# Two graph layers on one core: another order of head sums, V products, key dots and the load of x on VectorE

## The chip, the cores and the metric

The kernel runs on one core of one Trainium2 chip. The metric is device microseconds of one execution. All arithmetic is float32. The engines are called as the profile calls them: PE is TensorE (PEld its weight loads), DVE VectorE, ACT ScalarE, POOL GpSimd, SP SyncE, which here only issues DMAs. Each engine works through its own instructions strictly in the order in which they are written; between engines, semaphores make an instruction wait for what it needs.

## What is computed

64 graphs of 256 nodes with 512 features go through two layers:

```python
# layer 0: one head
feat = einsum('bnh,oh->bno', x, fc_w) + fc_b
q, k = feat . q_w + q_b, feat . k_w + k_b
masked = leaky_relu(q + k^T + (1 - adj) * -1e9, 0.01)
x1 = einsum('bnm,bmh->bnh', softmax(masked), feat) + x
# layer 1: eight heads of 64
Q, K, V = x1 @ W_q + b_q, x1 @ W_k + b_k, x1 @ W_v + b_v
scores = Q K^T / 8 + a[i] + c[j] + b_g + log(adj + 1e-9)     # a, c: x1 . w_g
out = softmax(scores) V + x1
```

## The kernel before

Two graphs (512 tokens) make a group; there are 32 groups. The loop at the end (from line 1155) takes one `step` a group, and each step works on three to four groups at once: `f`, whose features of layer 1 are computed now; `a`, the group before it, which is in its attention (scores, softmax, weighted sum); `d`, the one before that, whose last outputs leave; and `n`, the next, whose x and adj are loaded and whose layer-0 weights are prepared. The order of everything is written out by hand: a step is a list of strings such as `A("both:0 parts:0")`, where the letter names the group and each word a method with its arguments. The order of the words is the order on every engine that a method uses.

What matters for the change:

- **Block products.** The 512x512 products with the weights (Q, K, V as `pq`, `pk`, `pv`, and `pf` in layer 0) are each made of seven products of half blocks instead of eight (class `Product`, lines 383 to 468). `p1` opens an accumulator in PSUM; ACT copies it out (`keep_1`). `p6` and `p5` add to it, and each time ACT copies it out again (`s2`, `s4`); `p3` adds to it once more and ACT reads the block of the result. `p2` opens one of its own, and `p7` a third. DVE makes the other three blocks of the result: `sum_00` from p2 and the first copy, `sum_11` from p7 and `s4`, `sum_10` from the third after `p4` has added to it, and `s2`. So `p4` may only add when `sum_11` has read the third accumulator, and `p3` only when ACT has copied `s4`. All matmuls of these products have line 404, the sums line 432, the copies 418 and 421.
- **Tokens' sums.** `xsum:0` to `xsum:3` (line 369, tile t1b) and in layer 0 `ysum:0` to `ysum:3` (line 344, tile tb) are the differences of blocks that products 5, 6, 7 and 4 take. `copy:n` are copies on ACT.
- **Head sums.** In attention each of the four units u (graph, half of the heads) has two tiles e of exponentials. `both:u` (line 875) adds them into one tile `es`, `parts:u` transposes it into `est` (line 904) and reduces it to partial row sums (line 905). `est` takes the buffer e0, which also holds the layer-0 weights of the next group in another part of the step. `totals`, `ratios` (line 926), `turn` (966), `divide` (986), `complete` (994) and `store` (1027) finish an output of one graph; `turn_residual` (832) transposes the residual into `xb`, which has two buffers, freed when the stores from it have landed.
- **x and adj.** x has one buffer. The four `keys` dots (line 508, jc) are the last readers of x of the group f; then `load_x` (line 200) fetches x of the group n, and its first readers are the four `dot_q` (jq). `spread` sends the results through DRAM and back to all partitions (qrow), for `weights:0` and `weights:1` (lines 593, 597, and the exponential on ACT, line 598), which make the layer-0 weights in e0. adj has one buffer, filled at the start of a step in four DMAs (line 195) and read by `adjt` (line 551) in its last third; ACT makes the mask from it (lines 559, 560).
- **x1 transposed.** As each quarter of x1 is done (line 490), `send` (lines 781, 785) transposes it in blocks and writes it to DRAM, and `fetch` (line 793) reads it back in four DMAs as x1T, which Q, K and V are made from.
- **PSUM.** There are eight banks; the scores (line 850) of a step use all eight twice, and each takes a bank that an earlier tile has left.

Of the kernel before, what the change touches and what calls it, by code (L numbers as in the profile page):

```python
# [10 lines left out]
F32 = mybir.dt.float32  # L11
# [6 lines left out]
P = 128  # L18
# [7 lines left out]
def kernel(  # L26
# [65 lines left out]
    NB, N, D = x.shape  # L92
# [4 lines left out]
    NC = D // P  # L97
# [15 lines left out]
    both = [i for i, a in enumerate(act_sets.SETS) if a.name == "natural_log_exp_and_others"]  # L113
    nc.scalar.add_instruction(
        mybir.InstLoadActFuncSet(
            name=nc.get_next_instruction_name(), act_func_set_id=both[0], ins=[], outs=[]
# [47 lines left out]
    def fast():  # L164
        main = ExitStack()
        with main:
            one = main.enter_context(tc.tile_pool(name="one", bufs=1))
# [350 lines left out]
            class Group:  # L518
# [378 lines left out]
                def parts(self, u):  # L897

                    g, (gr, hg), nb = self.g, divmod(u, 2), NC * N // B
                    if hg == 0:  # L900
                        self.part_all = two.tile([P, ALL], F32, tag="part", name=f"part_{g}_{gr}")
                        self.part = self.part_all[:, 0 : 2 * nb].rearrange("p (a m) -> p a m", a=2)
                    turned = one.tile([P, NC * N], F32, tag="e0", name=f"est_{g}_{u}")
                    nc.vector.transpose(turned, self.esum[u].rearrange("p a b i -> p (a b i)"))  # L904
                    nc.vector.tensor_reduce(  # L905
                        self.part[:, hg, :], turned.rearrange("p (m c) -> p m c", c=B),
                        AX.X, ALU.add,
                    )
# [137 lines left out]
            def attention_and_layer_0(D, A, F, X):  # L1046

                A("scores:0 scores:1 scores:2 scores:3")
                F("add_tiles parts_0")
                A("factor:0:0 factor:0:1 factor:1:0 factor:1:1")  # L1050
                A("factor:2:0 factor:2:1 factor:3:0 factor:3:1")
                F("mix:0 mix:1 recip mix:2 mix:3 ysum:0")
                D("ratios:1 divide:1")
                A("residual:1")
                F("ysum:1")
                D("complete:1 store:1")
                F("ysum:2 pf.p1 pf.keep_1 pf.p2 pf.p6 pf.sum_00 begin send:0:0 fetch:0:0 ysum:3")
                A("turn_residual:1 both:0 parts:0")
                F("pf.p7 pf.p5 pf.p3 pf.add_01 pf.sum_11 send:1:1")
                A("attend:0")  # L1060
                F("pf.sum_01 send:0:1 fetch:1:1 fetch:0:1")
                A("both:1 turn:0 attend:1 parts:1")
                F("copy:0 pf.p4 pf.sum_10 send:1:0 fetch:1:0")
                F("pq.p1 pq.keep_1 pk.p1")
                A("totals:0")
                F("pk.keep_1 pv.p1 pv.keep_1")

            def check_ranges():

                in_range(NG - NR // 2, NG, "last")  # L1070
                pk = bank("pok")
                nc.tensor.transpose(pk[0:1, 0:P], checked["all"], ident)

                def flag_ready():
                    oks = one.tile([1, 2], F32, tag="oks", name="oks")
                    nc.vector.tensor_reduce(oks[:, 0:1], pk[0:1, 0:P], AX.X, ALU.min)
                    nc.vector.tensor_copy(flag, oks[:, 0:1])

                return flag_ready
# [3 lines left out]
            def step(d, a, f, n, check):  # L1083


                def of(group):
                    def issue(pieces):
                        for piece in pieces.split():
                            name, *args = piece.split(":")
                            if group is None:  # L1090
                                continue
                            target = group
                            if "." in name:
                                part, name = name.split(".")
                                target = getattr(group, part)
                            getattr(target, name)(*map(int, args))
                    return issue

                D, A, F, X = of(d), of(a), of(f), of(n)
                f.older = d  # L1100
                X("load_adj")
                if a is not None:
                    attention_and_layer_0(D, A, F, X)
                else:
                    f.features_first()
                    F("pq.p1 pq.keep_1 copy:0 pk.p1 pk.keep_1 pv.p1 pv.keep_1")
                F("xsum:0 xsum:1 xsum:2 pq.p6")
                A("ratios:0 both:2 parts:2")
                F("keys:2 keys:3 keys:0 keys:1")
                X("load_x")  # L1110
                F("pq.p7 pq.p2 pq.sum_00 xsum:3")
                check()
                F("pq.p5 pk.p6 pq.sum_11 pq.p3")
                A("divide:0")
                X("dot_q:0 dot_q:1 dot_q:2 dot_q:3 spread")
                F("pq.p4 pq.sum_10 copy:1 copy:2")
                A("complete:0 store:0 turn:1 both:3 parts:3")
                F("pk.p7 pk.p5 pk.sum_11 residual:0")
                X("adjt")
                F("pk.p2 pk.sum_00")  # L1120
                X("dot_k:0 dot_k:1")
                F("pk.p3 pk.p4 pk.sum_10")
                X("dot_k:2 dot_k:3")
                F("turn_residual:0")
                if n is None:
                    A("totals:1 ratios:1 divide:1 complete:1 store:1")
                    F("residual:1 turn_residual:1")

                    F("pv.p2 pv.p6 pv.sum_00 scores:0 scores:1 scores:2 scores:3")
                    F("pv.p7 factor:0:0 factor:0:1 factor:1:0 factor:1:1 both:0 both:1")  # L1130
                    F("pv.p5 pv.sum_11 pv.p3 sums_1:0 pv.p4 pv.sum_10")
                    F("factor:2:0 factor:2:1 ratios_t:0 ratios_r:0 factor:3:0 factor:3:1")
                    F("attend:0 finish:0 sums_of_e:1 attend:1")
                    F("ratios_t:1 ratios_r:1 finish:1")
                    check_ranges()()
                    return
                X("mask add_eps")
                F("pv.p2 pv.p6")
                X("weights:0")
                F("pv.p7 pv.p5")  # L1140
                X("weights:1")
                F("pv.sum_00 pv.p3 pv.sum_11 pv.p4 pv.sum_10")

            with tc.manual_schedule(engines=ENGINES):
                f = Group(0)
                f.x, f.a = x_0, adj_0

                warm = bank("warm")
                for n in range(6):
                    nc.tensor.matmul(warm[:, 0:P], lhsT=ident, rhs=ident, start=True, stop=True)  # L1150
                columns(rows_0, cols_0, "cols_0")
                rows_qk = rows_of_x()
                k_constant = constant()
                d, a, a_w = None, None, {}
                for g in range(NG):
                    n = Group(g + 1) if g + 1 < NG else None

                    def check():

                        if d is not None and (d.g % NR == NR - 1 or d.g == NG - NR // 2 - 1):  # L1160
                            in_range(d.g // NR * NR, d.g + 1, f"{d.g}")

                    step(d, a, f, n, check)
                    d, a, f = a, f, n
# [215 lines left out]
```

## Time and profile before

| what | value |
|---|---|
| median of three runs | 2486.52 us |
| lowest, highest | 2484.86, 2499.46 us |
| profiled execution: device time | 2491.2 us |
| its span, first to last instruction | 2489.4 us |
| its granted TensorE clock, mean | 0.983 |
| DMA, mean over the span | 66 GB/s |

The costliest groups of the page, for the durations (line, engine, operation, result and operands, shapes, count; busy us, mean ns of one; idle time before them and what ended it):

```profile
L867 DVE TENSOR_TENSOR e<-e,am 128x1024 f32<-128x1024 f32 x256 | 293.4, 1218 | 0.0
L404 PE MATMUL pk<-t1b,wk 128*128 128x256 f32 x512 | 147.2, 438 | 92.7 <-DVE kT L432 92.7
L904 DVE STREAM_TRANSPOSE est<-es 128x1024 f32<-128x1024 f32 x124 | 153.1, 1235 | 3.2
L905 DVE TENSOR_REDUCE part<-est 128x32 f32<-128x1024 f32 x124 | 151.3, 1220 | 4.2
L875 DVE TENSOR_TENSOR es<-e,e 128x1024 f32<-128x1024 f32 x126 | 152.6, 1212 | 0.4
L508 DVE CUSTOM_DVE_ANT_0 jq<-x,wq_row 128x512 f32<-128x512 f32 x128 | 88.5, 692 | 51.1 <-DMA x<-in_x_dram 47.8
```

The granted clock is the share of its full speed that the TensorE was given. Ends of matmuls are modelled; their starts tell more. An idle time is put down to whatever came last.

### The profile page before, as it was taken

Reading aid. Unit: us, or ns where it says so; the run is one execution under the profiler, and the core shown is the slowest. Engines: PE = TensorE matmul, PEld = TensorE weight load, DVE = VectorE, ACT = ScalarE, POOL = GpSimd, SP = SyncE. Lnnn points to the kernel's source line nnn. Section 1 sums busy time; section 2 is a strip of 40 time slices with the busy share of each in tenths; the row PEclk is TensorE's granted clock in tenths of the full one; section 3 lists DMA queues with packets and bytes.
Section 4 is the critical chain, followed back from the end, with each engine's and each line's share of the span. In section 5 each row is a group of like instructions: output and inputs, shape, how many; then the busy total and the mean of one; then the engine's idle time right before and its main releaser. Section 6 shows DMA issues by size and latency. Waiting matters only on the chain.

```text
span 2489.4 us, 33742 instructions
## 1 busy us (share of the span) xinstructions
PE 2338.5 (94%) x12554; PEld 1924.0 (77%) x12554; DVE 2155.1 (87%) x3212; ACT 1086.1 (44%) x2121; POOL 130.4 (5%) x120
## 2 busy tenths in 40 slices
PE   9999999999999999999999999999999999999997
PEld 6877777777787777877777877778777787777875
DVE  6788888888888898888889888898988988889897
ACT  3444344443444443444434444344444344443443
POOL 0000000000000000000000000000000000000000
PEclk9999999999999999999999999999999999999999
DMA  4122322223322223222232222322222322223222
GB/s 123 47 56 64 81 67 57 56 64 81 75 66 56 60 68 81 67 58 56 64 81 68 55 61 58 81 74 67 60 60 64 81 63 61 55 64 81 66 50 36
DMA packets 517266, 163.85 MB, mean 66 GB/s; under 512 B 415188, under 2 KB 478696, under 8 KB 517096
## 3 DMA queue, kind: packets, MB, share of 16 engines
q1 hardware_dynamic: 514440, 160.32, 27.1%
q8 instruction: 101, 1.65, 0.3%
q10 hardware_dynamic: 2656, 1.31, 0.2%
q14 instruction: 69, 0.57, 0.1%
HBM read 95.43 MB, written 66.12 MB: 65 GB/s over the span
## 4 chain that ended last, share of the span: by engine, by line
PE 45%; DVE 34%; DMA 12%; issue 3%; SPq 3%; ACT 1%; DVEq 0%; POOL 0%; ACTq 0%; POOLq 0%
PE pv L404 11%; PE y L678 9%; PE sc L850 9%; PE pf L404 7%; DMA x<-in_x_dram 7%; DVE est L904 4%; DVE es L875 4%; DVE jq L508 3%; PE pk L404 3%; DVE part L905 3%; DVE x L490 2%; PE pq L404 2%; SPq L793 2%; DMA xd<-xt 2%; PE oT L888 2%
## 5 line engine op out<-in xcount | busy, mean ns | idle before, releaser
L859 ACT ACTIVATE e<-sc,c 128x512 f32<-128x512 f32 x512 | 299.3, 735 | 69.9 <-PE sc L850 69.9
L867 DVE TENSOR_TENSOR e<-e,am 128x1024 f32<-128x1024 f32 x256 | 293.4, 1218 | 0.0
L484 POOL TENSOR_TENSOR pf_s<-pf_s,x 128x512 f32<-128x512 f32 x93 | 126.9, 1364 | 2274.8 <-ACT pf_s L483 2217.5
L404 PE MATMUL pk<-t1b,wk 128*128 128x256 f32 x512 | 147.2, 438 | 92.7 <-DVE kT L432 92.7
L850 PE MATMUL sc<-qT,kT 64*128 64x256 f32 x2048 | 230.7, 380 | 0.0
L888 PE MATMUL oT<-e,v 128*64 128x256 f32 x2048 | 230.0, 383 | 0.0
L678 PE MATMUL y<-e,x 128*128 128x256 f32 x992 | 228.8, 384 | 0.0
L850 PEld LDWEIGHTS sc<-qT,kT 64*128 64x128 f32 x2048 | 196.1, 187 | 32.4 <-issue 10.6
L678 PEld LDWEIGHTS y<-e,x 128*128 128x128 f32 x992 | 183.6, 190 | 32.7 <-ACT e L859 10.3
L888 PEld LDWEIGHTS oT<-e,v 128*64 128x64 f32 x2048 | 144.9, 138 | 81.1 <-issue 12.5
L404 PEld LDWEIGHTS pk<-t1b,wk 128*128 128x128 f32 x512 | 108.7, 218 | 121.8 <-DVE kT L432 105.2
L895 ACT COPY oTs<-oT 128x512 f32<-128x512 f32 x128 | 71.9, 587 | 262.1 <-DVE osb L966 133.6
L421 ACT ACTIVATE pq_s<-pq,cols 128x256 f32<-128x256 f32 x192 | 80.5, 471 | 238.9 <-DVE qT L432 126.5
L904 DVE STREAM_TRANSPOSE est<-es 128x1024 f32<-128x1024 f32 x124 | 153.1, 1235 | 3.2
L905 DVE TENSOR_REDUCE part<-est 128x32 f32<-128x1024 f32 x124 | 151.3, 1220 | 4.2
L875 DVE TENSOR_TENSOR es<-e,e 128x1024 f32<-128x1024 f32 x126 | 152.6, 1212 | 0.4
L483 ACT ACTIVATE pf_s<-pf,recip 128x256 f32<-128x256 f32 x186 | 77.4, 467 | 153.3 <-PE pf L404 153.3
L432 DVE TENSOR_TENSOR v<-pv,pv_s 128x512 f32<-128x512 f32 x96 | 64.1, 687 | 89.7 <-PE pv L404 84.9
L508 DVE CUSTOM_DVE_ANT_0 jq<-x,wq_row 128x512 f32<-128x512 f32 x128 | 88.5, 692 | 51.1 <-DMA x<-in_x_dram 47.8
L404 PE MATMUL pv<-wv,t1b_c 128*128 128x256 f32 x512 | 131.8, 403 | 0.0
L818 ACT ACTIVATE xv<-x1T,cols 128x256 f32<-128x256 f32 x256 | 109.1, 498 | 50.1 <-DVE osb L966 46.2
L418 ACT COPY pk_s<-pk 128x512 f32<-128x512 f32 x96 | 56.3, 586 | 168.5 <-PE pk L404 95.3
(175 smaller groups left out, 4597.0 us busy)
## 6 DMA issues: line engine op xcount, KB each, us to landing
x<-in_x_dram SPq DMA_DIRECT2D x32, 1024.0 KB, 5.1
xd<-xt SPq DMA_DIRECT2D x124, 256.0 KB, 2.0
x1T<-xd SPq DMA_DIRECT2D x496, 64.0 KB, 2.0
out_dram<-xb SPq DMA_DIRECT2D x248, 128.0 KB, 3.1
adj<-in_adj_dram SPq DMA_DIRECT2D x128, 128.0 KB, 3.6
qrow<-q SPq DMA_DIRECT2D x31, 256.0 KB, 4.0
fc_nat<-in_L_gnn_fc_w_dram ACTq DMA_DIRECT2D x4, 256.0 KB, 4.4
wq<-in_L_gnn_W_q_dram SPq DMA_DIRECT2D x1, 1024.0 KB
```

The lines of the kernel that those rows point to most:

```text
L404: nc.tensor.matmul(o, lhsT=lk[:, ts(m, P)] if len(lk.shape) == 2 else lk[:, m], rhs=rk, start=(start and m == 0 and k == 0), stop=(m == 1 ...
L484: nc.gpsimd.tensor_tensor(s, s, self.out(o, k), ALU.add)
L508: nc.vector.tensor_tensor_reduce(out=junk, in0=src, in1=w_row, scale=1.0, scalar=init, op0=ALU.mult, op1=ALU.add, accum_out=dst,)
L678: nc.tensor.matmul(y[:, ts(gr, N)], lhsT=self.x[:, gr * TPG + j, ts(c, P)], rhs=self.e0[:, j, gr, :], start=(gr == 0 and j == 0), stop=(gr ...
L818: nc.scalar.activation(self.xv[:, c].rearrange("p (t a m) -> p t a m", t=TPG, m=B), self.x1T[:, c // 2, gr].rearrange("p (a t c m) -> p c ...
L850: nc.tensor.matmul(sc[par][:, pr, :], lhsT=self.kT[rows, 2 * hg + pr, ts(t, P)], rhs=self.qT[rows, 2 * hg + pr, ts(gr, N)], start=True, st ...
L859: nc.scalar.activation(e[:, par], sc[par], AF.Exp, bias=self.c[:, t : t + 1], scale=SCALE)
L867: nc.vector.tensor_tensor(ef, ef, self.am[:, jc, u // 2, :].unsqueeze(1).to_broadcast([P, 4, N]), ALU.mult,)
L875: nc.vector.tensor_tensor(self.esum[u], self.e[u, 0], self.e[u, 1], ALU.add)
L888: nc.tensor.matmul(oT[par * HD : (par + 1) * HD, pr, :], lhsT=self.v[:, gr * TPG + jc, ts(h, HD)], rhs=self.e[2 * gr + hg, jc][:, par, pr, :],
L904: nc.vector.transpose(turned, self.esum[u].rearrange("p a b i -> p (a b i)"))
L905: nc.vector.tensor_reduce(self.part[:, hg, :], turned.rearrange("p (m c) -> p m c", c=B), AX.X, ALU.add,)
```

## The change

Four things move in the step; no instruction is added or taken away. The sum of the last head unit, `both:3 parts:3`, goes from its place behind `turn:1` (ahead of pk.sum_11) to the end of the step, between pv.sum_00 and pv.sum_10; in the last step, which has no next group, it stays where it was. Since e0 holds the next group's layer-0 weights by then, its transposed tile takes the buffer of adj instead. The key dots and the load of x go ahead of `ratios:0 both:2 parts:2`. The V products run as 6 7 5 2 3 4 instead of 2 6 7 5 3 4, with their sums in the order 11, 00, 10. And `turn_residual:1` goes behind `both:0 parts:0`.

```diff
-                    turned = one.tile([P, NC * N], F32, tag="e0", name=f"est_{g}_{u}")
+                    tag = "adj" if u == 3 else "e0"
+                    turned = one.tile([P, NC * N], F32, tag=tag, name=f"est_{g}_{u}")
...
-                A("turn_residual:1 both:0 parts:0")
+                A("both:0 parts:0 turn_residual:1")
...
-                A("ratios:0 both:2 parts:2")
                 F("keys:2 keys:3 keys:0 keys:1")
                 X("load_x")
+                A("ratios:0 both:2 parts:2")
                 F("pq.p7 pq.p2 pq.sum_00 xsum:3")
...
-                A("complete:0 store:0 turn:1 both:3 parts:3")
+                A("complete:0 store:0 turn:1")
+                if n is None:
+                    A("both:3 parts:3")
                 F("pk.p7 pk.p5 pk.sum_11 residual:0")
...
                 X("mask add_eps")
-                F("pv.p2 pv.p6")
+                F("pv.p6 pv.p7")
                 X("weights:0")
-                F("pv.p7 pv.p5")
+                F("pv.p5 pv.p2")
                 X("weights:1")
-                F("pv.sum_00 pv.p3 pv.sum_11 pv.p4 pv.sum_10")
+                F("pv.sum_11 pv.p3 pv.p4 pv.sum_00")
+                A("both:3 parts:3")
+                F("pv.sum_10")
```

## The prediction

> **What bounds the kernel now.** The page's engine totals come first: PE is busy for 94% of the span, so most of the time is matmul and a change of order on VectorE can only win what PE spends waiting. So I read the waits of PE next, then the timelines at the longest one.
>
> ```profile
> PE 2338.5 (94%) x12554; PEld 1924.0 (77%) x12554; DVE 2155.1 (87%) x3212; ACT 1086.1 (44%) x2121; POOL 130.4 (5%) x120
> ```
>
> The waits of PE (total us, times, longest) name the places:
>
> ```profile
> PE pk L404 <- DVE kT L432: 92.7, 31, 3.6
> PE pv L404 <- ACT pv_s L418: 21.6, 32, 0.7
> PE pq L404 <- DMA x1T<-xd: 7.0, 8, 1.4
> PE pq L404 <- DVE t1b L369: 6.5, 10, 0.9
> ```
>
> One wait is most of it: once a step, a K product (pk, line 404) waits some 3 us for a VectorE sum into kT. The timeline around one such place, first PE, then DVE (start, duration, what; idle before it in brackets), shows who is late:
>
> ```profile
> 1210.71 1.89 PE L404 MATMUL pk<-x1T,k_s 128*128 128x256 f32 x8
> 1215.19 3.56 PE L404 MATMUL pk<-t1b,wk 128*128 128x256 f32 x8 [2.59 <-DVE kT L432]
> 1218.58 1.89 PE L404 MATMUL pv<-wv,t1b_c 128*128 128x256 f32 x8
> ...
> 1226.33 1.99 PE L404 MATMUL pv<-v_s,t1b_c 128*128 128x256 f32 x8 [0.68 <-ACT pv_s L418]
> ```
>
> ```profile
> 1202.03 1.22 DVE L986 TENSOR_TENSOR osb<-osb,recip 128x1024 f32<-128x1024 f32 x1
> 1204.98 0.69 DVE L508 CUSTOM_DVE_ANT_0 jq<-x,wq_row 128x512 f32<-128x512 f32 x1 [1.73 <-DMA x<-in_x_dram]
> ...
> 1210.82 1.18 DVE L875 TENSOR_TENSOR es<-e,e 128x1024 f32<-128x1024 f32 x1
> 1212.04 1.25 DVE L904 STREAM_TRANSPOSE est<-es 128x1024 f32<-128x1024 f32 x1
> 1213.32 1.22 DVE L905 TENSOR_REDUCE part<-est 128x32 f32<-128x1024 f32 x1
> 1214.45 0.68 DVE L432 TENSOR_TENSOR kT<-pk,pk_s 128x512 f32<-128x512 f32 x1
> ```
>
> pk.p4 adds into the bank that pk.sum_11 (1214.45) has to read first. That sum stands behind `both:3 parts:3` (1210.82 to 1214.45: 3.63 us) and, further up, behind 1.73 us in which DVE waits for x. Its own operands were there by 1209.8, when ACT's pk_s copy ended. So DVE was 4.6 us late.
>
> The stall has a second price. Two-microsecond windows of PE (length, busy and count, granted clock, DMA share, GB/s) show it:
>
> ```profile
> 1214.00:1216.00 2.00, 0.81 (x2) 0.74 1.02 151
> 1216.00:1218.00 2.00, 2.00 (x6) 0.50 0.10 16
> 1218.00:1220.00 2.00, 2.00 (x10) 0.90 1.14 178
> 1220.00:1222.00 2.00, 2.00 (x11) 1.00 0.55 69
> ```
>
> After the gap PE runs some 3.4 us at half clock: eight matmuls take 3.56 instead of 1.89. In steps without this the way from the pk.p4 that had to wait to the next restart, pv.p3, is 9.58 us (1752.53 to 1762.11); in 18 of 31 steps it is longer, mostly 11.26, and the excesses add up to 31.5 us.
>
> **The change, part by part.** I count from S, the first score matmul of a step (1229.98 here). Without stalls PE's order then gives pk.p2 at S+54.9, pk.p3 +56.7, pk.p4 +58.4, six V products of 1.73 each, the next S at about +70.7.
>
> *Keys and load of x ahead of `ratios:0 both:2 parts:2`.* Nothing is added; the four key dots keep their 2.9 us. The load is issued after the last of them, so earlier by what it now passes: reciprocals 0.73, es 1.26, transpose 1.28, reduce 1.14, 4.4 us. It takes 5.1 to land, and DVE waits 1.7 to 2.1 for it now (47.8 us, 30 times). All of that goes. On SP no other issue lies between the old and the new place; only the last fetch of x1T comes closer (rival D).
>
> *`both:3 parts:3` behind pv.sum_00.* 3.63 us leave the way to pk.sum_11. Walked from S with the row durations, DVE reaches it at S+54.9 and now waits there 0.8 for ACT's pk_s (pk.p5 ends at +55.1, the copy takes 0.6); the sum is done at +56.4, two microseconds before pk.p4 wants it. pk.sum_10 then waits for pk.p4 itself (+60.3). From there DVE runs: sum 0.6, two dots 1.5, xb 1.2, weights:0 1.9 and weights:1 1.9, V sums 0.6 and 0.7, then the moved three 3.6: pv.sum_10 starts at +72.3, that is 1.6 after the next S, where it was 0.1 after it. Its cover is the scores: the bank that pv.sum_10 frees is the eighth score bank, first wanted at S+2.9; freed at S+2.3. If that cover went, PE would wait the difference. Further on, DVE starts the eight e factors 1.5 later; tb (ysum:1) then ends at S+16.8, pf.p6 wants it at +17.8, and the 1.24 that DVE now waits for POOL's pf_s takes up the rest.
>
> *est_3 in the adj buffer.* SP issues the adj loads only after the moved reduce (S+1.6, before: S-13.7). Behind them on SP stand store:1 (S+17.8) and the sends (S+20 on); four issues of 2.8 us and 3.6 to land are over by S+9, and adj is read at S+56. Cost zero; it has 45 us of cover.
>
> *V products 6 7 5 2 3 4.* pv.p3 waited 0.68 for ACT's copy after p5, every step. Now p2 (1.73) stands between and covers copy and handover, so 0.68 goes in 31 steps (the last has its own order). But that copy stands on ACT behind the exponential of weights:0. By the rows of this step (1218.78 pk.sum_10 to 1224.71 end of that exponential, and 0.58 for the copy) it is done at S+60.3+6.5=66.8; p3 wants it at +67.0. That is the narrowest place of the walk, 0.2 us. p4 needs pv.sum_11, done at +67.8, wanted at +68.8.
>
> *`turn_residual:1` behind `both:0 parts:0`.* It waited 44.1 us in all (about 1.0 a step) for the store that frees xb. The three moved ahead (3.65) cover that, so the x sums, sends and fetches behind it come 1.0 earlier. Little hangs on it, as PE waits only 7.0 for x1T and 6.5 for t1b in all; these 13.5 and some 5 for ACT's copies are my bound for the further gain, zero the other end. I take zero, as new waits of a few tenths are as likely.
>
> **The sum.** The pk stalls: 92.7 less 0.5 in the last step, whose order stays: 92.2. The pv stalls: 31 x 0.68 = 21. The half clock: 31.5, if no other gap takes its place; stalls that remain are short, and after those of 0.68 to 1.44 the rows show no slowed matmul. Together 144.7 us of the profiled execution's 2491.2 (span 2489.4): 2346.5. The median of the runs is 4.7 below it, so 2342; I say 2340. The check: the mean distance from one pk stall to the next is 76.73 us ((2367.19-141.91)/29), and a step without half clock, 834.30 to 909.12, less its stalls 2.91 and 0.68, is 71.2; thirty steps at most 166 less, 2320.
>
> [...]
>
> **Rivals.** *A: the waits move to the V products.* The 0.2 at pv.p3, the 0.6 at the eighth score bank and the 1.0 at pf.p6 and pv.p4 are thin. If DVE or ACT come 1 to 2 us later than walked, PE loses 0.8 to 1.8 in 30 steps: 2364 to 2394. For it: everything from pk.p4 to the exponential of weights:0 is a chain without slack. Against: each price is a row. *B: DVE becomes the bound.* It is occupied 68.6 of the 76.85 us of this step (idle in brackets: 8.24). With the waits that stay (POOL 1.24, yT 0.48, kT 0.47, pq_s 0.37) 71.2, just PE's own; 2 us more a step would give 2400. *C: no change (2462 to 2511).* The sum would have to be late for another reason; against it, its operands stood ready for 4.6 us. *D: slower.* The load of x starts at S+40.9; the last fetch of x1T is issued by +39.9 and lands at about +41.7, and pq.p2 wants it at +42.5. If the megabyte overtakes it, and takes the 8.6 us of the longest landing of x in the trace, the fetch lands at +49.5: 7.0 us of stall and 1.7 of half clock, against 4.8 gained: 30 x 3.9 = 117 more, 2600. It decides from an overtaking load of over 5 us; against it, the fetch is in flight a microsecond ahead.
>
> **Chances and range.** Forecast 0.68 (its own range 2318 to 2355), A 0.17, B 0.06, C 0.05, D 0.04. The range 2315 to 2390 takes in the forecast and nearly all of A. Faster by over 1% (what a measurement here can tell) 0.91, within 1% 0.05, slower 0.04.
>
> **What would show it.** After: PE's wait for kT near zero but for the last step, likewise pv for pv_s; granted clock 0.99 or more; no wait of jq for x and of xb for a store; steps of 71 to 72 us; DVE's longest wait at pk's sums. I am wrong if PE shows a new wait at pv.p3, pv.p4, the scores or pq.p2 of over 1 us a step, or if half-clock stretches stay although the gaps are gone.

## The result and the profile after

The changed kernel takes 2330.46 us (median of 4 runs, 2327.61 to 2332.77); the kernel before, beside it, 2489.6 (2484.86 to 2499.46). The ratio is 0.9355, 95% interval 0.9323 to 0.9388. The profiled execution took 2331.2 us with a span of 2329.4 and a granted clock of 0.998.

First the engine totals of the changed kernel's page, then its waits of PE (total us, times, longest):

```profile
PE 2293.2 (98%) x12554; PEld 1902.1 (82%) x12554; DVE 2202.7 (95%) x3212; ACT 1080.2 (46%) x2121; POOL 125.5 (5%) x120
```

```profile
PE pok L1073 <- DVE okp_last L1044: 7.0, 1, 7.0
PE pq L404 <- DVE t1b L369: 3.9, 6, 1.2
PE pq L404 <- DMA x1T<-xd: 3.9, 5, 0.9
PE pq L404 <- ACT pq_s L421: 3.8, 9, 0.5
PE pv L404 <- ACT pv_s L418: 2.0, 4, 0.7
...
PE pk L404 <- DVE kT L432: 0.5, 1, 0.5
```

The wait of pk for kT, 92.7 us before, is one of 0.5 in the last step. That of pv for pv_s fell from 21.6 to 2.0, and that of pq for x1T, t1b and ACT from 17.0 to 11.6. The timeline of the changed kernel at the place of the former stall, PE and then DVE:

```profile
1204.27 1.89 PE L404 MATMUL pk<-x1T,k_s 128*128 128x256 f32 x8
1206.00 1.89 PE L404 MATMUL pk<-t1b,wk 128*128 128x256 f32 x8
1207.73 3.62 PE L404 MATMUL pv<-v_s,t1b 128*128 128x256 f32 x16
...
1218.18 7.18 PE L850 MATMUL sc<-qT,kT 64*128 64x256 f32 x64
```

```profile
1203.37 0.69 DVE L432 TENSOR_TENSOR kT<-pk,pk_s 128x512 f32<-128x512 f32 x1 [0.20 <-ACT pk_s L418]
...
1207.93 0.69 DVE L432 TENSOR_TENSOR kT<-pk,pk_s 128x512 f32<-128x512 f32 x1 [0.69 <-PE pk L404]
...
1216.16 1.22 DVE L875 TENSOR_TENSOR es<-e,e 128x1024 f32<-128x1024 f32 x1
1217.41 1.25 DVE L905 STREAM_TRANSPOSE est<-es 128x1024 f32<-128x1024 f32 x1
1218.70 1.22 DVE L906 TENSOR_REDUCE part<-est 128x32 f32<-128x1024 f32 x1
1219.83 0.68 DVE L432 TENSOR_TENSOR v<-pv,pv_s 128x512 f32<-128x512 f32 x1
```

pk.p4 follows pk.p3 without a gap, because pk.sum_11 (1203.37) is done two microseconds earlier. It is now DVE that waits, 0.69 us, for pk.p4. The moved head sum lies over the last V product and the start of the scores, and pv.sum_10 starts 1.65 us after them.

The two-microsecond windows there (length, PE busy and count, granted clock, DMA share, GB/s) show full clock:

```profile
1206.00:1208.00 2.00, 2.00 (x11) 1.00 1.08 159
1208.00:1210.00 2.00, 2.00 (x11) 1.00 0.04 8
```

Between the two profiled executions 160.0 us went: 92.2 of pk stalls, 19.6 of pv, 5.4 of these pq waits, and the 31.5 of half clock in the steps: ten-microsecond windows of the whole span show the clock below 1.00 only in the last twenty. That is 148.7. Of the 11 that are left some 5 are half clock as well: by the granted clock over the whole traces it cost 41.6 us before (34.1 of them in the steps) and 5.0 after, 36.6 less and not 31.5. The other 6 were not followed up.

### The profile page after: what moved, and what is told of

The parts are those of the page before. It is cut to its first block, busy times and chain, and to the rows that moved or that the text cites. A ratio compares the mean times of both kernels' runs of the same rounds, so it can differ in the third digit from the quotient of the medians.

```text
span 2329.4 us, 33749 instructions
## 1 busy us (share of the span) xinstructions
PE 2293.2 (98%) x12554; PEld 1902.1 (82%) x12554; DVE 2202.7 (95%) x3212; ACT 1080.2 (46%) x2121; POOL 125.5 (5%) x120
## 3 DMA queue, kind: packets, MB, share of 16 engines
q8 instruction: 101, 1.65, 0.3%
## 4 chain that ended last, share of the span: by engine, by line
PE 56%; DVE 31%; DMA 5%; issue 4%; SPq 2%; ACT 1%; DVEq 0%; POOL 0%; ACTq 0%; POOLq 0%
PE pk L404 11%; PE pq L404 10%; PE pf L404 9%; PE pv L404 9%; PE y L678 6%; PE sc L850 5%; DVE e L867 5%; PE oT L888 5%; DVE est L905 2%; DVE es L875 2%; DVE x L490 2%; DMA xd<-xt 2%; DVE jc L508 2%; DVE tb L344 2%; DVE e L593 1%
## 5 line engine op out<-in xcount | busy, mean ns | idle before, releaser
L484 POOL TENSOR_TENSOR pf_s<-pf_s,x 128x512 f32<-128x512 f32 x93 | 121.9, 1311 | 2118.2 <-ACT pf_s L483 2049.5
L678 PEld LDWEIGHTS y<-e,x 128*128 128x128 f32 x992 | 183.6, 190 | 32.7 <-ACT e L859 10.3
L404 PE MATMUL pq<-x1T,wq 128*128 128x256 f32 x512 | 122.8, 383 | 4.5 <-DMA x1T<-xd 3.9
L404 PE MATMUL pv<-wv,t1b_c 128*128 128x256 f32 x512 | 122.7, 382 | 0.0
L404 PE MATMUL pk<-t1b,wk 128*128 128x256 f32 x512 | 121.1, 379 | 0.5 <-DVE kT L432 0.5
L404 PE MATMUL pq<-t1b,wq 128*128 128x256 f32 x512 | 121.4, 380 | 0.0
L404 PE MATMUL pv<-wv,t1b 128*128 128x256 f32 x512 | 121.1, 379 | 0.0
L404 PE MATMUL pk<-t1b,k_s 128*128 128x256 f32 x512 | 120.9, 379 | 0.0
```

Of the source, the lines that this page charges most:

```text
L404: nc.tensor.matmul(o, lhsT=lk[:, ts(m, P)] if len(lk.shape) == 2 else lk[:, m], rhs=rk, start=(start and m == 0 and k == 0), stop=(m == 1 ...
L484: nc.gpsimd.tensor_tensor(s, s, self.out(o, k), ALU.add)
L678: nc.tensor.matmul(y[:, ts(gr, N)], lhsT=self.x[:, gr * TPG + j, ts(c, P)], rhs=self.e0[:, j, gr, :], start=(gr == 0 and j == 0), stop=(gr ...
```

## The experiments

Eleven kernels. Ratios are to the kernel before, run beside them; the changed kernel's own is 0.9355.

### One part alone

The head sum alone: its tile in the adj buffer, and its place as in the change, with the V order of before:

```diff
-                A("complete:0 store:0 turn:1 both:3 parts:3")
+                A("complete:0 store:0 turn:1")
+                if n is None:
+                    A("both:3 parts:3")
...
-                F("pv.sum_00 pv.p3 pv.sum_11 pv.p4 pv.sum_10")
+                F("pv.sum_00 pv.p3 pv.sum_11 pv.p4")
+                A("both:3 parts:3")
+                F("pv.sum_10")
```

> Only the last head sum moves behind the V sums (with its tile in the adj buffer); V order, keys and residual as before. Theory (VectorE is late at pk.sum_11 and 3.63 us of lateness are enough for a stall of 3.07 on average): the pk stalls go to under 10 us, the half clock goes with them, the 0.68 at pv.p3 and the wait for x stay; gain 92 + 31 = 123, about 2366 us. Rival (each of the two causes, 3.63 and 1.73, owns its share of the gain): 0.68 x 124 = 84 gained, about 2405 us, with pk stalls of about 1 us left.

2379.58 us, ratio 0.9553 (0.952 to 0.9585): 111 us gained. The pk stalls are all gone, and the clock is 0.997, so the threshold holds against shares. But 12 us of the expected gain are missing. Waits of PE in this kernel:

```profile
PE pv L404 <- ACT pv_s L418: 28.4, 32, 2.0
PE pq L404 <- DMA x1T<-xd: 9.7, 14, 1.7
PE pq L404 <- DVE t1b L369: 7.2, 13, 0.8
```

All three are longer than before (21.6, 7.0, 6.5), by 10 us together: VectorE is now late elsewhere.

The keys and the load of x alone:

```diff
-                A("ratios:0 both:2 parts:2")
                 F("keys:2 keys:3 keys:0 keys:1")
                 X("load_x")
+                A("ratios:0 both:2 parts:2")
```

> Only the key dots and the load of x move ahead of the third head sum. Theory: VectorE comes 1.6 us earlier to pk.sum_11 (its wait for x goes), pk stalls of about 1.5 us instead of 3.07 are left: 48 gained, 2441 us; if gaps of 1.5 us no longer halve the clock, 31 more, 2410 us. Rival (the wait for x is only replaced by another wait ahead of pk.sum_11): no gain, 2489 us.

2413.7 us, ratio 0.9695 (0.9663 to 0.9727). The wait for x is gone, and the pk stall is 44.2 us in 31 times, most of them 1.3:

```profile
951.74 1.99 PE L404 MATMUL pk<-t1b,wk 128*128 128x256 f32 x8 [1.29 <-DVE kT L432]
```

The eight matmuls after that gap take 1.99 us, at full clock, and the mean clock is 0.996. That is the second of the two numbers given, 2410. So this part alone brings 76 us by the ratio: 48 of pk stalls, and most of the rest half clock that no longer comes.

The V order alone, and `turn_residual:1` alone:

```diff
-                F("pv.p2 pv.p6")
+                F("pv.p6 pv.p7")
                 X("weights:0")
-                F("pv.p7 pv.p5")
+                F("pv.p5 pv.p2")
                 X("weights:1")
-                F("pv.sum_00 pv.p3 pv.sum_11 pv.p4 pv.sum_10")
+                F("pv.sum_11 pv.p3 pv.p4 pv.sum_00")
+                F("pv.sum_10")
```

> Only the order of the V products and their sums changes. Theory: the 0.68 us at pv.p3 goes in 31 steps, 21 us, 2469 us; the pk stalls stay at 92. Rival (TensorE is not what this stage waits for, VectorE's round is): the pk stall grows by what pv.p3 saved, no gain, 2489 us.

2476.57 us, ratio 0.994 (0.9923 to 0.9956): 15 of the 21. The pk stalls stay at 92.5 and those of pv fall to 3.6, as the theory has it. The mean clock of the profiled run is 0.978 instead of 0.983 (25 stretches at half clock in the steps instead of 18), so more half clock took some of it back.

```diff
-                A("turn_residual:1 both:0 parts:0")
+                A("both:0 parts:0 turn_residual:1")
```

> Only turn_residual:1 moves behind both:0 parts:0. By the record's sum (little hangs on it): 0 to 13 us, 2476 to 2489 us. Rival (VectorE's lateness runs through the whole step, so that the 1.0 us saved here comes out at pk.sum_11): pk stalls of 2.1 instead of 3.07, 30 us, 2460 us.

2475.08 us, ratio 0.9952 (0.9925 to 0.9979): 12 us by the ratio, of 0 to 13 expected. The rival fell: the pk stalls are 93.0. But the wait for the store was gone (5.0 us, once, in place of 44.1), so where did its microsecond go? DVE in this kernel, and POOL beside it:

```profile
1012.30 2.29 DVE L875 TENSOR_TENSOR es<-e,e 128x1024 f32<-128x1024 f32 x1
```

```profile
1012.05 1.46 POOL L484 TENSOR_TENSOR pf_s<-pf_s,x 128x512 f32<-128x512 f32 x1 [1.90 <-DVE xt L781]
```

The sum of `both:0`, now the next in line, takes 2.29 us instead of 1.18: it starts under GpSimd's add and ends 1.08 after it, as if it had waited for its end. In 30 of its 126 executions es is stretched so, 32.7 us in all; in the kernel before in 5, 2.2 us in all. The wait for the store had covered GpSimd's add. A wait that looked like one of DMA was to three quarters also one for another engine.

### One part taken back from the changed kernel

Each edit is the reverse of the part above; the head sum goes back with its tile in e0.

> The changed kernel with the last head sum back ahead of pk.sum_11. Theory (a threshold: only VectorE's total lateness against 4.6 us counts, and the other moves take 1.7 and 1.0 of it): pk stalls of about 0.7 us, no half clock, about 22 us slower than the changed kernel, 2353 us. Rival (this move is the main part of the gain): its 92 us of stall come back, about 2425 us.

2395.36 us, ratio 0.9599 (0.9577 to 0.9621). Between the two: the pk stall is 42.2 us and not some 20. Here too es is stretched, in 29 executions by 31.6 us, which the walk from S had not counted; with that microsecond the walk's 0.7 becomes at most 1.8, and the 1.4 measured (42.2 in 30 steps) lies between. With the head sum no longer there to fill it, DVE's wait for the V products is 61.9 us (4.2 in the changed kernel). The pk stall alone is not the whole loss, which is some 61 us by the ratios: PE's wait for pv_s is back to 15.6 us (2.0 in the changed kernel), and the half clock, of which the expectation had none, costs 11.6 instead of 5.0.

> The changed kernel with keys and load of x back behind the third head sum. Theory (threshold, pk.sum_11 has 2.0 us to spare): VectorE waits 1.5 us for x again, TensorE notices nothing, 2331 us, within 5. Rival (the parts add up): 1.6 x 30 = 48 slower, 2379 us.

2365.66 us, ratio 0.9475 (0.945 to 0.95): some 30 us slower, where the theory had none. There is no pk stall, as said. PE of this kernel, and DVE, at one of the places where it loses:

```profile
1229.60 1.89 PE L404 MATMUL pv<-wv,t1b_c 128*128 128x256 f32 x8
1233.39 2.81 PE L404 MATMUL pv<-v_s,t1b_c 128*128 128x256 f32 x8 [1.91 <-ACT pv_s L418]
1236.00 2.80 PE L404 MATMUL pv<-wv,t1b 128*128 128x256 f32 x8
```

```profile
1215.93 0.69 DVE L508 CUSTOM_DVE_ANT_0 jq<-x,wq_row 128x512 f32<-128x512 f32 x1 [1.97 <-DMA x<-in_x_dram]
...
1229.03 1.24 DVE L832 STREAM_TRANSPOSE xb<-xv 128x1024 f32<-128x1024 f32 x1 [1.35 <-DMA out_dram<-xb]
...
1232.06 1.24 DVE L593 SCALAR_TENSOR_TENSOR e<-qrow,kq,e 128x256 f32<-128x256 f32 x2
```

DVE waits for x, and here later for the store that frees xb as well, so the weights come late; the copy that pv.p3 needs stands on ACT behind their exponential. In all PE waits 24.2 us for pv_s, 26 times. It is rival A of the prediction at the place named narrowest there, and a gap of 1.91 us halves the clock again (two groups of 2.8 us).

> The changed kernel with the old order of V products and sums (head sum still just ahead of pv.sum_10). Theory: 0.68 us at pv.p3 comes back in each step, 21 us, 2351 us. Rival (other slack takes it): 2331 us.

2347.95 us, ratio 0.9411 (0.9391 to 0.9432): some 14 us slower than the changed kernel by the ratios, where 21 were expected; the intervals of the two ratios allow both. pv waits 21.9 us for pv_s, as expected.

> The changed kernel with turn_residual:1 back ahead of both:0 parts:0. Theory: VectorE waits 0.9 us a step for the store again, the x1T sums come later and TensorE waits up to 0.6 us for t1b: 0 to 20 us slower, 2331 to 2350 us; no pk stall. Rival (lateness reaches pk.sum_11): 30 us or more, 2360 us, with pk stalls.

2355.53 us, ratio 0.9445 (0.9421 to 0.947): some 22 us slower than the changed kernel, a little over the expected end. DVE waits 27.2 us for the store, PE 10.3 for x1T and 10.8 for t1b (3.9 and 3.9 with the move), and not at pk. The move is worth 12 us alone and 22 in the company of the others; by their intervals (5 to 19, some 12 to 32) that difference is not shown.

### What is left, and GpSimd's adds

In the changed kernel the stretched instruction is another one: tb, in 60 of 124 executions, 58.0 us in all. One experiment takes ysum:3 out from under GpSimd's second add; one has four of the sixteen fetch DMAs of a step issued by ACT; one does both:

```diff
-                F("ysum:2 pf.p1 pf.keep_1 pf.p2 pf.p6 pf.sum_00 begin send:0:0 fetch:0:0 ysum:3")
+                F("ysum:2 pf.p1 pf.keep_1 pf.p2 pf.p6 pf.sum_00 begin send:0:0 fetch:0:0")
                 A("both:0 parts:0 turn_residual:1")
-                F("pf.p7 pf.p5 pf.p3 pf.add_01 pf.sum_11 send:1:1")
+                F("ysum:3 pf.p7 pf.p5 pf.p3 pf.add_01 pf.sum_11 send:1:1")
```

> The changed kernel with ysum:3 (two SBUF operands) taken out from under GpSimd's second add and put behind turn_residual:1. Theory (a VectorE sum of two SBUF operands that starts while GpSimd's add runs waits for its end): the third and fourth form of tb no longer both take 1.55 to 1.76; this ysum:3 takes 0.69, and both:0, which now starts about when GpSimd is ready, either holds GpSimd back (1.2 us) or is itself stretched to 2.3. In the first case VectorE is 0.9 us earlier and 0 to 10 us are gained: 2320 to 2330. Rival (tb is slow for its own reasons, the first read of yT by VectorE say): ysum:3 stays at 1.55 wherever it stands, 2330.

2331.66 us, ratio 0.9339 (0.9325 to 0.9354): no gain. Its DVE and POOL:

```profile
1237.87 1.76 DVE L344 TENSOR_TENSOR tb<-yT 128x512 f32<-128x512 f32 x1
...
1241.20 2.10 DVE L875 TENSOR_TENSOR es<-e,e 128x1024 f32<-128x1024 f32 x1
...
1246.92 0.65 DVE L344 TENSOR_TENSOR tb<-yT,tb 128x512 f32<-128x512 f32 x1
```

```profile
1237.74 1.34 POOL L484 TENSOR_TENSOR pf_s<-pf_s,x 128x512 f32<-128x512 f32 x1 [62.82 <-ACT pf_s L483]
1240.96 1.27 POOL L484 TENSOR_TENSOR pf_s<-pf_s,x 128x512 f32<-128x512 f32 x1 [1.89 <-ACT pf_s L483]
```

ysum:3 is back at 0.65; es, which now starts 0.24 us after the start of the second add, takes 2.10. It is the place that decides, not the instruction: the rival falls.

```diff
-                def fetch(self, o, k):
+                def fetch(self, o, k, act=0):
...
-                        nc.sync.dma_start(dst[q], src[q])
+                        (nc.scalar if act else nc.sync).dma_start(dst[q], src[q])
...
-                F("pf.sum_01 send:0:1 fetch:1:1 fetch:0:1")
+                F("pf.sum_01 send:0:1 fetch:1:1:1 fetch:0:1")
```

> The changed kernel with the four DMAs of fetch:1:1 issued by ScalarE instead of SyncE. Theory (what TensorE still waits for in the Q products is the queue of eight issues on SyncE, 3.7 to 5.5 us): t1b's waits for x1T (7.4 us) and TensorE's for x1T and t1b (7.8) fall to a few us, 2322 to 2328. Rival (the late landings are the DMAs themselves): no change, 2330; or ScalarE, blocked behind these issues, comes late to its copies and TensorE waits for pq_s, 2335 to 2345.

2328.75 us, ratio 0.9326 (0.931 to 0.9342). PE's waits for x1T and t1b are 7.5 against 7.8: the queue of issues was not what is left. The theory falls.

> Both of the two edits together. Theory: 2318 to 2328, the better of the two or a little more. Rival: no change, 2330.

2327.61 us, ratio 0.9321 (0.9306 to 0.9336). The interval overlaps that of the changed kernel; no version here is shown to be faster than it.

## Why the prediction was right

The time, 2330, lies in the forecast's own range, ten below the number given.

*Where PE waits and why.* Right: both parts that take VectorE's lateness away at pk.sum_11 end or halve the pk stall when done alone (0 and 44 us), and the two that don't leave it at 92.5 and 93.0.

*The walk from S.* DVE was put at pk.sum_11 at S+54.9 with 0.8 of waiting, pv.sum_10 at +1.6 after S; measured, DVE is there at +55.8 (S is 1147.35 for this one) and waits 0.20, and pv.sum_10 stands at +1.65. The end of the walk was right. Its middle was not: before, the x sums (pf.add_01) came at S+26.8; by the prediction's terms, 1.5 later and then earlier by the waits of 1.24 for pf_s and 1.0 for the store, they would come at some +26.1. They came at +27.3 (S is 1218.18 here). DVE and POOL of the changed kernel:

```profile
1235.88 1.75 DVE L344 TENSOR_TENSOR tb<-yT 128x512 f32<-128x512 f32 x1
...
1239.21 1.55 DVE L344 TENSOR_TENSOR tb<-yT,tb 128x512 f32<-128x512 f32 x1
...
1245.50 0.83 DVE L490 SCALAR_TENSOR_TENSOR x<-pf,recip,x 128x256 f32<-128x256 f32 x2
```

```profile
1235.71 1.37 POOL L484 TENSOR_TENSOR pf_s<-pf_s,x 128x512 f32<-128x512 f32 x1 [62.80 <-ACT pf_s L483]
1238.94 1.27 POOL L484 TENSOR_TENSOR pf_s<-pf_s,x 128x512 f32<-128x512 f32 x1 [1.86 <-ACT pf_s L483]
```

The step that failed is "the 1.24 that DVE now waits for POOL's pf_s takes up the rest": the wait went, but the sums that moved under GpSimd's adds were stretched, 58 us in 60 executions. It cost no time, as pk.sum_11 was still done two microseconds before pk.p4. It is also part of why the expectations for the kernels with less to spare (keys back, head sum back) were too good; that for the keys, besides, looked at pk.sum_11 alone and left out the 0.2 at pv.p3.

*Thin places.* The 0.2 at pv.p3 held: 2.0 us of waits there. With the keys back it gave way. So rival A was the right rival, and the keys, which at pk alone would not have been needed, are what keeps it away.

*The other terms.* 21 forecast at pv.p3, 19.6 measured. DVE's wait for x, 47.8 us before, is gone, and so is its wait for the store, but for 6.6 us of 44.1; it never waits for adj. For `turn_residual:1` I took zero, between zero and 18 us; x1T, t1b and ACT's copies for pq gave 5.4, and taking the move back costs 22. That is the term that was too small.

*The half clock.* 31.5 us were counted in and went. Over all profiled executions of this study, the first and the last 60 us of each left out, of 83 gaps of 1.0 to 1.9 us none was followed by half clock; of 107 gaps from 1.9 to 3.6 us 68 were, the shortest 1.91. Among these the length alone does not decide: in the kernel before, half clock followed a gap of 2.20 us (at 2290.07) and not one of 3.56 (at 2056.43). The granted clock of that trace shows 18 stretches at half clock in the steps. Each begins a whole multiple of 3.41 us after the one before, and 16 of them last 3.41 us, two 6.83. If that trace is cut into windows by this grid, half clock followed all 18 windows at full clock in which PE was idle for 1.97 us or more, and none with 1.92 or less. The gap of 3.56 lay across a boundary, with 1.79 us in one window and 1.77 in the next.

*Rivals B, C, D.* DVE is busy 95% of the span, close to bounding, as B had it, but PE is at 98%. C fell with the stall. D: the Q products wait for x1T 3.9 us in all, less than the 7.0 before, so the earlier load of x did not overtake the fetch.

## What to carry to other kernels

A stall of the busy engine is a threshold on the other engine's lateness: what is taken out of that engine's way pays until the stall, here some 3 us, is gone, and more than that pays only as margin. So parts measured one by one don't add up (by the ratios 111, 76, 15 and 12 us alone, 214 in sum, and 161 together). Walk the whole round with row durations and write down the margin at each handover; the one with 0.2 us was where the first missing part showed. And price a stall by its half clock as well: here a third again on top of the gap, refunded when the gaps became shorter than 1.9 us.

## What the hardware showed

Two VectorE sums of two SBUF operands, tb (128x512) and es (128x1024), were stretched when they started while GpSimd added into pf_s. In the changed kernel 60 tb and one es start so; each tb ended 0.55 us after GpSimd did and the es 1.08, most of their own full time. tb takes mostly 1.55 to 1.76 us there instead of 0.69; es took 2.1 to 2.3 instead of 1.2 in the kernels with `turn_residual:1` alone and with ysum:3 moved, so the stretching moved with the place. What in GpSimd's add holds them up is not shown. The price is hidden in the trace: it stands as busy time of VectorE, not as a wait. The reduces (part<-est), which read one operand, are not stretched here: 31 of them start under an add in the changed kernel and take 1.22 us as elsewhere.
